# A selective-scan kernel whose work between two batches is put out by a model of the engines

## The chip, the cores and the metric

The kernel runs on one core of a Trainium2 chip. Its time is the device time of one execution in microseconds (us); the runs shown of before have a median of 16161.84 us. A core has a matrix engine (TensorE, PE in the profile), three elementwise engines (VectorE or DVE, ScalarE or ACT, GpSimd or POOL) and a queue that issues most transfers (SyncE, SP). Each engine takes its instructions in the order of its own program.

## The reference: what is computed

The input x is (4, 64, 64, 96): four images of L = 4096 positions and 96 channels. Four layers follow each other, and the change touches the first two, which have the same skeleton:

```
xg   = GroupNorm(x)                       # 32 groups of 3 channels
xi,z = split(xg @ in_proj_w.T)            # 192 channels each
xc   = silu(depthwise_conv3x3(xi) + b)
for each of 4 directions kd:              # four orders of the 4096 positions
    dt, B, C = projections of xc in that order
    h[t] = h[t-1] * exp(dt[t] * A) + dt[t] * xc[t] * B[t]     # 192 channels x 16 states
    y_kd[t] = sum over states of h[t] * C[t], plus D * xc[t]
y = sum over kd of w_kd * y_kd, brought back to the image's order
y = LayerNorm(y over the 192 channels) * ln_g + ln_b
y = y * silu(z)
```

Layer 0 walks the image along diagonals and by radius, with weights w_kd for each position, and ends with `x + y @ out_proj_w.T`. Layer 1 walks rows and columns, forwards and backwards, without weights; its y goes on to an out-projection and a feed-forward block. Layers 2 and 3 (attention, a quantised feed-forward, an FFT mixer) are not touched.

## The kernel before, in words

All arithmetic is in f32. `Stream.run` treats the first two layers as one row of eight batches (two layers times four images). A batch is 4 directions of 4 segments of 1024 positions, each of 6 channel blocks and 4 groups of states. The steady work of a batch is: VectorE enters (line 725) and scans (line 732), ScalarE takes exponentials (L720), GpSimd multiplies by C (L742), and TensorE gathers over states (`collect`, L753) and spreads the inputs (L712). Idle matmuls on zeros (`keep_busy`, L776) lie ahead of the collects; they write the column tile that the collect's first part writes too, and the collect's second part writes another tile.

Before a batch can be scanned, its **front** must have run (`front`, from L259): it loads the image in strips of 1024 positions, takes GroupNorm statistics (L284 on VectorE, L291 and L297 on TensorE), loads the strips again, normalises them (L310), and for each of the four strips projects the inner half by channels (L318, copied to a padded tile at L324), projects z by tokens (L330, Silu at L335, stored to `z_tok`), convolves (L356), applies Silu (L370), transposes to tokens (L376, copies L380), stores `x_tok` (L391) and the product with D's weights `dx_tok` (L393 on GpSimd, store L398).

The convolution is 108 matmuls of 32x32 weights (diagonals) with 512 columns for each strip: 9 taps, 3 blocks of 32 channels in each half, and 4 positions `at` (two halves times two groups of 8 rows). `tile_position=(blk * 32, at * 32)`: the block picks the row group of the matrix array and the position the column group.

After a batch has been scanned, its **merge** runs (`merge`, from L407) in 8 chunks of 512 positions: it fetches the four directions' y (L422 by SP, or L426 by 64 indirect transfers of GpSimd, for directions 2 and 3 of layer 0), sums them (L448 with weights, L450 without), takes LayerNorm statistics (L460, L461), applies norm and affine and multiplies by z, in rows of tokens (L472 to L474 on VectorE in layer 0; in layer 1 VectorE normalises at L478 and GpSimd does three passes, L480 and L481), transposes (L492), copies (L497 on ScalarE), and then projects and adds x (L504, L506; layer 0) or stores `y1` (layer 1).

Between batch q-1 and batch q no scan runs: `flush` ends the last collects, and then `between(q)` puts out front(q+1) and merge(q-1), step by step in turn, with the front left out in every third turn. Only after that the program spreads the inputs of batch q (`spread_u`, L712) and scans on. The order in each engine's program is exactly the order in which these generators put it out (`manual_schedule`); nothing moves it later. SP and GpSimd issue transfers in that order too, so a transfer that waits for its data holds the ones behind it.

At the start the order is: front(0) alone, then the fetch of the first segment (`fetch`, L559, 52 transfers) and its preparation (`prepare`, L605 to L690), the loads of the first rows of B, C and delta, then `between(0)`, which is front(1) alone, then the first scan. At the end merge(7) runs alone.

Of the kernel before, what the change touches and what calls it, by code (L numbers as in the profile page):

```python
# [21 lines left out]
B = 4  # L22
# [122 lines left out]

class Layer:


    def __init__(self, s, a, pre, x_in):
# [9 lines left out]
        self.ln_g, self.ln_b = (k.t(w, [128, DI], pre + n) for n in ("ln_g", "ln_b"))  # L159
        nc.sync.dma_start(self.ln_g, a[pre + "ln_g"].to_broadcast([128, DI]))  # L160
        nc.sync.dma_start(self.ln_b, a[pre + "ln_b"].to_broadcast([128, DI]))
# [58 lines left out]
class Stream:  # L220
# [38 lines left out]
    def front(self, bt):  # L259

        k, nc, lay = self.k, self.nc, bt.lay
        x = lay.x_in[:, bt.b, :]
        bt.x_tok = k.t(self.dram, [L, DI], "x_tok")
        bt.dx_tok, bt.z_tok = (k.t(self.dram, [L, DI], n, bufs=3) for n in ("dx_tok", "z_tok"))
        stats = k.t(self.tmp, [C, NCH, 6], "gn_stats")
        strips = L // SEG
        tiles, pads = {}, {}

        def load(s):
            xs = k.t(self.core, [C, SEG], "da", bufs=4)  # L270
            nc.sync.dma_start(xs, x[:, s * SEG : (s + 1) * SEG])
            return xs

        def load_strip(s):

            tiles[s] = load(s), k.t(self.tmp, [C, 2, HW], "halo", bufs=2)
            for n, row in enumerate((s * 16 - 1, s * 16 + 16)):
                if 0 <= row < HW:
                    nc.sync.dma_start(tiles[s][1][:, n], x[:, row * HW : (row + 1) * HW])

        for c in range(strips):
            xs = load(c)
            for j in range(2):
                nc.vector.bn_stats(stats[:, 2 * c + j, :], xs[:, j * CH : (j + 1) * CH])  # L284
            yield
        for s in range(2):
            load_strip(s)
        mv, gn, d = (k.t(self.tmp, [C, n], t) for n, t in ((2, "gn_mv"), (2, "gn"), (1, "gn_d")))
        nc.vector.bn_aggr(mv, stats.rearrange("p c s -> p (c s)"))
        ps = k.t(self.ps, [C, 1], "m")  # L290
        nc.tensor.matmul(ps, self.gavg, mv[:, 0:1], start=True, stop=True)  # L291
        yield
        nc.vector.tensor_copy(gn[:, 0:1], ps)
        nc.vector.tensor_sub(d, mv[:, 0:1], gn[:, 0:1])
        nc.vector.scalar_tensor_tensor(d, d, d, mv[:, 1:2], op0=ALU.mult, op1=ALU.add)
        ps = k.t(self.ps, [C, 1], "m")
        nc.tensor.matmul(ps, self.gavg, d, start=True, stop=True)  # L297
        yield
        k.rstd(gn[:, 1:2], ps)

        def project(s):

            pad = pads[s] = self.spare()[:C].rearrange("p (h r w) -> p h r w", h=2, r=18)
            nc.gpsimd.memset(pad[:, :, :, 0 : HW + 2 : HW + 1], 0.0)
            r0 = s * 16
            xs, halo = tiles.pop(s)
            has = [r0 > 0, r0 + 16 < HW]
            edge = slice(0 if has[0] else 1, 2 if has[1] else 1)
            for v in (xs, halo[:, edge]):
                nc.vector.tensor_scalar(v, v, gn[:, 0:1], gn[:, 1:2], op0=ALU.subtract, op1=ALU.mult)  # L310
            for n in range(2):
                if not has[n]:
                    nc.gpsimd.memset(pad[:, :, n * 17, :], 0.0)
            for part in range(3):
                v = xs[:, part * CH : (part + 1) * CH] if part < 2 else halo[:, edge].rearrange("p r w -> p (r w)")
                ps = k.t(self.ps_t, [C, 2, CH], "t")[:, :, : v.shape[1]]
                for half in range(2):
                    nc.tensor.matmul(ps[:, half], lay.in_w[:, half * C : (half + 1) * C], v, start=True, stop=True)  # L318
                yield
                if part < 2:  # L320
                    rows = slice(1 + part * 8, 9 + part * 8)
                else:
                    rows = slice(edge.start * 17, 18, 17) if edge.stop == 2 else slice(0, 1)
                nc.scalar.copy(pad[:, :, rows, 1 : 1 + HW], ps.rearrange("p h (r w) -> p h r w", w=HW))  # L324
            stores = []
            for j in range(2):
                ps = k.t(self.ps_t, [128, 2, CH], "t")[:, :, : 2 * DI].rearrange("p a (b d) -> p a b d", d=DI)
# [12 lines left out]
            for to, z in stores:  # L340
                nc.sync.dma_start(to, z)
# [1661 lines left out]
```

## Time and profile before

| | us |
|---|---|
| runs shown: median (lowest to highest) | 16161.84 (16144.28 to 16188.49) |
| the profiled execution's own time | 16120.49 |
| its span | 16118.7 |
| first scan (L732) begins | 392.5 |
| gaps without a scan between batches 0-1, 1-2, 2-3, 3-4 (merge of layer 0) | 206.8, 206.4, 209.0, 209.5 |
| gaps 4-5, 5-6 (merge of layer 1, front of layer 1) | 187.1, 185.0 |
| gap 6-7 (merge alone) | 129.8 |
| last scan ends | 12878.7 |
| granted TensorE clock, mean of the span | 0.861 |

The share of busy time over the whole span is PE 83%, DVE 80%, POOL 62%, ACT 51%. It is an average over stages with different limits, so the gaps and the start are read by themselves, by the busy time in stretches. A matmul in f32 is two passes of the array in the records, and each is counted as one instruction.

### The profile page before, as it was taken

What the parts mean: (1) busy time and instruction counts of PE and PEld (TensorE: products, weight loads), DVE (VectorE), ACT (ScalarE), POOL (GpSimd) and SP (SyncE); (2) the same over time, 40 slices, a digit from 0 to 9 for tenths busy, and PEclk for the clock granted to TensorE, in tenths of its full rate; (3) what the DMA queues carried; (4) which work ended last, traced back from release to release, by engine and by line L of the source; (5) the groups of instructions that cost most, each with busy time, mean ns of one, the idle gap of its engine ahead of it and who ended that gap; (6) DMA issues with size and microseconds to landing.
All of it is one profiled execution on the core that took longest, in us unless ns stands there. A gap on an engine that the chain in (4) does not pass through costs nothing. (4 is left out here: it accounts for less than half of the span.)

```text
span 16118.7 us, 190118 instructions
## 1 busy us (share of the span) xinstructions
PE 13409.0 (83%) x70447; PEld 4873.8 (30%) x70447; DVE 12944.4 (80%) x9690; ACT 8242.0 (51%) x14120; POOL 9957.1 (62%) x5025
## 2 busy tenths in 40 slices
PE   6888788878887888788878887888688869998877
PEld 3222222222222222222222222222222234443344
DVE  1989798979897989799979997999899956565555
ACT  3656465646564656466545654655466523332334
POOL 1888588858885888577757775777677730000123
PEclk8888888988888888888878888888788879998878
DMA  3333533353334333433343334333433320000132
GB/s 113 107 114 109 157 109 110 114 160 104 115 107 151 107 115 109 152 109 119 115 143 120 111 114 154 107 115 107 139 112 122 101 65 18 11 17 13 37 84 69
DMA packets 927836, 1675.23 MB, mean 104 GB/s; under 512 B 103206, under 2 KB 617515, under 8 KB 923132
## 3 DMA queue, kind: packets, MB, share of 16 engines
q1 hardware_dynamic: 890044, 1587.51, 31.7%
q0 software_dynamic: 36864, 75.55, 1.5%
q8 instruction: 558, 9.14, 0.2%
q14 instruction: 370, 3.03, 0.1%
HBM read 1308.00 MB, written 354.75 MB: 103 GB/s over the span
## 5 line engine op out<-in xcount | busy, mean ns | idle before, releaser
L742 POOL TENSOR_TENSOR hc<-h,bc 128x1024 f32<-128x1024 f32 x3072 | 7183.5, 2357 | 2112.6 <-DVE h L732 1681.4
L732 DVE TENSOR_TENSOR_SCAN h<-da,state,t 128x1024 f32<-128x1024 f32 x2304 | 5270.8, 2328 | 13.7 <-ACT da L720 9.6
L753 PE MATMUL y<-hc,gather_y 128*32 128x512 f32 x12288 | 4281.9, 689 | 671.4 <-POOL hc L742 506.2
L725 DVE TENSOR_TENSOR t<-u,bc 128x1024 f32<-128x1024 f32 x3072 | 3599.5, 1217 | 998.8 <-PE u L712 998.3
L720 ACT ACTIVATE da<-dts,L_A_logs 128x1024 f32<-128x1024 f32 x3072 | 3488.1, 1147 | 730.8 <-DMA dts<-dt_dram 438.4
L712 PE MATMUL u<-dtu,spread 32*128 32x512 f32 x3072 | 1881.2, 739 | 374.2 <-DVE t L725 370.2
L776 PE MATMUL y<-L_diag,zeros 96*32 96x256 f32 x5218 | 1751.8, 466 | 0.0
L732 DVE TENSOR_TENSOR_SCAN h<-da,t 128x1024 f32<-128x1024 f32 x768 | 1711.7, 2268 | 9.1 <-ACT da L720 8.4
L753 PEld LDWEIGHTS y<-hc,gather_y 128*32 128x32 f32 x12288 | 802.1, 117 | 2465.9 <-issue 1266.7
L644 PE MATMUL m<-xs,proj 96*128 96x512 f32 (+1 forms) x2048 | 1017.8, 620 | 116.7 <-ACT dt L653 60.4
L681 ACT COPY dt<-m 96x512 f32<-96x512 f32 x512 | 296.7, 579 | 1533.5 <-PE m L676 1533.5
L712 PEld LDWEIGHTS u<-dtu,spread 32*128 32x128 f32 x3072 | 597.9, 215 | 1440.1 <-issue 1101.2
L776 PEld LDWEIGHTS y<-L_diag,zeros 96*32 96x32 f32 x5218 | 617.7, 132 | 1284.8 <-issue 1158.4
L1186 POOL MEMSET padp<- 128x2448 f32 x32 | 68.5, 2141 | 1413.1 <-PE d L1226 1405.0
L1262 DVE SCALAR_TENSOR_TENSOR hcv<-padv,taps,hcv 128x2048 f32<-128x2048 f32 x384 | 902.2, 2349 | 22.3 <-ACT padv L1203 8.6
L1226 PE MATMUL d<-padp,diag 32*32 32x512 f32 x25600 | 886.2, 601 | 2.0 <-ACT hcp L1241 2.0
L676 PE MATMUL m<-sp_z,ident 96*96 96x512 f32 x1024 | 535.1, 605 | 192.7 <-ACT sp_z L670 192.7
L636 POOL TENSOR_TENSOR dtu<-sp_z,dtu 96x1024 f32<-96x1024 f32 x256 | 604.1, 2360 | 72.5 <-ACT dtu L634 70.1
L648 ACT ACTIVATE sp_z<-m,L_dtb 96x512 f32<-96x512 f32 x512 | 348.8, 681 | 545.4 <-PE m L644 527.7
L1226 PEld LDWEIGHTS d<-padp,diag 32*32 32x32 f32 x25600 | 483.3, 103 | 372.1 <-issue 199.3
L797 ACT COPY spare<-m 128x512 f32<-128x512 f32 x384 | 225.0, 586 | 713.3 <-PE m L794 712.9
L644 PEld LDWEIGHTS m<-xs,proj 96*128 96x128 f32 (+1 forms) x2048 | 322.6, 177 | 822.8 <-issue 314.2
(276 smaller groups left out, 15542.6 us busy)
## 6 DMA issues: line engine op xcount, KB each, us to landing
bc<-bc_dram SPq DMA_DIRECT2D x1024, 512.0 KB
dts<-dt_dram SPq DMA_DIRECT2D x768, 512.0 KB
dt_dram<-dt SPq DMA_DIRECT2D x256, 384.0 KB
h<-y_tok SPq DMA_DIRECT2D x192, 384.0 KB
y_tok<-spare SPq DMA_DIRECT2D x64, 768.0 KB
z_tok<-z_rows SPq DMA_DIRECT2D x64, 384.0 KB
x_tok<-y_rows SPq DMA_DIRECT2D x32, 768.0 KB
dx_tok<-sp_z SPq DMA_DIRECT2D x32, 768.0 KB
```

The source lines that it names most:

```text
L636: rest = lambda half: nc.gpsimd.tensor_add(r[:, half], z[:, half], r[:, half])
L644: nc.tensor.matmul(ps, proj[:, src, to], xs[:, src, cols], start=src == 0, stop=src == 1)
L676: nc.tensor.matmul(ps, k.ident[:C, :C], term[:, half, cols], start=at == 0, stop=at == 2)
L712: self.nc.tensor.matmul(seg.u[:, cols], self.spread[rows, :], seg.dtu[rows, half, cols], start=True, stop=True)
L720: self.nc.scalar.activation(da, seg.dts[cb], AF.Exp, scale=seg.bt.lay.neg_a[:, seg.kd, g : g + 1])
L725: self.nc.vector.tensor_mul(gr.t, gr.seg.u, self.bc[:, 0, gr.sg, :])
L732: self.nc.vector.tensor_tensor_scan(gr.h[:, order], gr.da[:, order], gr.t[:, order], start, op0=ALU.mult, op1=ALU.add)
L742: self.nc.gpsimd.tensor_mul(gr.hc, gr.h, self.bc[:, 1, gr.sg, :])
L753: nc.tensor.matmul(seg.y[at : at + GC, :], self.gather_y, gr.hc[:, part * CH : (part + 1) * CH], start=gr.sg == 0, stop=gr.sg == NSG - 1, ...
L776: self.nc.tensor.matmul(gr.seg.y[at : at + GC, :256], self.zeros, gr.seg.bt.lay.diag.rearrange("p h t c -> p (h t c)")[:, :256], start=Fal ...
L1226: nc.tensor.matmul(pc[i][j * 32 : (j + 1) * 32, :], diag[mine, ON_PE.index(t), tap, :], pad[mine, j * 8 + dy : j * 8 + dy + 8, dx : dx + H ...
L1262: nc.vector.scalar_tensor_tensor(to, win, wt, to, op0=ALU.mult, op1=ALU.add)
```

## The change

`between` is replaced by `side_by_side`. Fronts and merges become many small threads that tell, before each step, which engine it needs and for how many microseconds by the code's own table (`yield "PE", 2.7`). `Plan.run` keeps for each engine the time at which the model has it free, and puts out next the thread that can start first. `Rings` keeps count of the buffers. Where the model sees TensorE idle for over 1 us it puts in an idle matmul of 384 columns (`fill`). The flush of the last collects is itself a thread (`ending`), at 1.2 us of the model's time, and fetches of directions 0 and 1 may stand ahead of it; they land in the halves of the tiles "dt" and "xs" of the segments, which hold z as well.

Five more things change with it. At the start, front(0) and front(1) are put out together, ahead of the first segment's fetch and preparation. A front loads the image once and keeps its four strips. z is projected by channels (two matmuls of 96x512 for each half strip, stored to `z_t` as [96, 2, L]). The convolution's loops go block, tap, position, and each block is one step of the plan. In the merge, VectorE normalises, the transposed result gets the affine on ScalarE (`Identity` with scale and bias for each channel), and the product with z follows by channels on VectorE. The pad's borders are cleared by VectorE. ln_g and ln_b are loaded as [96, 2].

```diff
+class Plan:
...
+    def run(self):
+        now = 0.0
...
+                start = max(th.at, self.free.get(th.wants[0], 0.0))
+                if best is None or (start, -th.ahead) < (best[0], -best[1].ahead):
+                    best = start, th
+            start, th = best
+            engine, us = th.wants
+            if engine == "PE" and self.fill:
+
+                for _ in range(int((start - self.free.get("PE", start)) / 1.0)):
+                    self.fill()
+            if engine != "none":
+                self.free[engine] = start + us
+                now = max(now, start)
+            th.at = start + us + (0.2 if us else 0.0)
+            self.current = th
+            th.wants = next(th.work, None)
+            if th.wants is None:
+                self.threads.remove(th)
+        self.current = None
...
-    def front(self, bt):
+    def front(self, bt, plan, rings, first=None):
...
+        if first:
+            yield lambda: first.to_project == 0
+        bt.to_project = L // SEG
...
+        bt.dx_tok = k.t(self.dram, [L, DI], "dx_tok", bufs=3)
...
+        mv, gn, d = (k.t(self.tmp, [C, n], t, bufs=2) for n, t in ((2, "gn_mv"), (2, "gn"), (1, "gn_d")))
+
+        def measure(s, st):
+            st.x = yield from take(self.core, [C, SEG], "da", 4)
+            yield "SP", 0.1
+            nc.sync.dma_start(st.x, x[:, s * SEG : (s + 1) * SEG])
+            yield "none", 2.5
+            yield "DVE", 1.4
+            for j in range(2):
+                nc.vector.bn_stats(stats[:, 2 * s + j, :], st.x[:, j * CH : (j + 1) * CH])
...
+        yield from plan.together([measure(s, st) for s, st in enumerate(strips)])
+        yield "DVE", 0.4
         nc.vector.bn_aggr(mv, stats.rearrange("p c s -> p (c s)"))
...
-        def project(s):
...
-            nc.gpsimd.memset(pad[:, :, :, 0 : HW + 2 : HW + 1], 0.0)
...
+        def project(s, st):
+
+            whole = yield from take(self.w, [128, 2 * 18 * (HW + 2)], "spare", 2)
+            pad = whole[:C].rearrange("p (h r w) -> p h r w", h=2, r=18)
...
+            xs, halo = st.x, st.halo
+            yield "DVE", 2.2
+            nc.vector.memset(pad[:, :, :, 0 : HW + 2 : HW + 1], 0.0)
+            for n in range(2):
+                if not has[n]:
+                    nc.vector.memset(pad[:, :, n * 17, :], 0.0)
             for v in (xs, halo[:, edge]):
                 nc.vector.tensor_scalar(v, v, gn[:, 0:1], gn[:, 1:2], op0=ALU.subtract, op1=ALU.mult)
-            for n in range(2):
-                if not has[n]:
-                    nc.gpsimd.memset(pad[:, :, n * 17, :], 0.0)
...
+                yield "ACT", 1.1 if part < 2 else 0.4
                 nc.scalar.copy(pad[:, :, rows, 1 : 1 + HW], ps.rearrange("p h (r w) -> p h r w", w=HW))
-            stores = []
-            for j in range(2):
-                ps = k.t(self.ps_t, [128, 2, CH], "t")[:, :, : 2 * DI].rearrange("p a (b d) -> p a b d", d=DI)
-                for t in range(4):
-                    at = j * CH + t * 128
-                    nc.tensor.matmul(
...
-                    )
...
+            def outer(j):
+                cols = slice(j * CH, (j + 1) * CH)
+                ps = yield from take(self.ps_t, [C, 2, CH], "t", 2)
+                yield "PE", 1.8
+                for half in range(2):
+                    w = lay.in_w[:, DI + half * C : DI + (half + 1) * C]
+                    nc.tensor.matmul(ps[:, half], w, xs[:, cols], start=True, stop=True)
+                z = yield from take(self.tmp, [C, 2, CH], "z_rows", 2)
+                yield "ACT", 1.1
                 nc.scalar.activation(z, ps, AF.Silu)
-                at = r0 * HW + j * CH
-                to = bt.z_tok[at : at + CH, :].rearrange("(j p) d -> p j d", p=128)
-                stores.append((to, z.rearrange("p a b d -> p (a b) d")))
-            yield
...
+                give(ps)
+                del ps
+                yield "SP", 0.1
+                at = s * SEG + j * CH
+                nc.sync.dma_start(bt.z_t[:, :, at : at + CH], z)
...
+            yield from plan.together([inner(part) for part in range(3)])
+            st.pad, st.whole = pad, whole
+            del pad, whole
+            yield from plan.together([outer(j) for j in range(2)])
...
+        def convolve(s, st):
+            yield lambda: st.pad is not None
...
+            two = yield from take(self.ps_t, [128, 2, CH], "t", 2)
+            one = yield from take(self.ps, [128, CH], "m", 1)
             ps = [two[:, 0, :], two[:, 1, :], one]
-            for tap in range(9):
-                dy, dx = divmod(tap, 3)
-                for blk in range(C // GC):
-                    mine = slice(blk * GC, (blk + 1) * GC)
+            for blk in range(C // GC):
+                yield "PE", 2.7
+                mine = slice(blk * GC, (blk + 1) * GC)
+                for tap in range(9):
+                    dy, dx = divmod(tap, 3)
                     for at in range(4):
                         half, j = divmod(at, 2)
                         nc.tensor.matmul(
                             ps[blk][at * GC : (at + 1) * GC, :],
                             lay.diag[mine, half, tap, :],
-                            pad[mine, half, j * 8 + dy : j * 8 + dy + 8, dx : dx + HW],
+                            st.pad[mine, half, j * 8 + dy : j * 8 + dy + 8, dx : dx + HW],
                             start=tap == 0,
                             stop=tap == 8,
                             tile_position=(blk * GC, at * GC),
                         )
-
-            for _ in range(3):
-                yield
-            xc = []
+            give(st.whole)
+            del st.whole, st.pad
...
+                yield "ACT", 0.7
                 nc.scalar.activation(xc[blk], ps[blk], AF.Silu, bias=lay.conv_b[:, blk : blk + 1])
...
             for blk, ps in enumerate((two[:, 0, :], two[:, 1, :], one)):
+                yield "PE", 1.2
                 for t in range(4):
                     nc.tensor.transpose(ps[:, t * 128 : (t + 1) * 128], xc[blk][:, t * 128 : (t + 1) * 128], k.ident)
...
+                yield "ACT", 0.8
                 for half in range(2):
...
-                nc.gpsimd.tensor_mul(dx, dx, rows)
+                nc.gpsimd.tensor_mul(dxs, dxs, flat)
...
-            for _ in range(3):
...
-        for s in range(strips + 1):
-            if s < strips:
-                yield from project(s)
-            if s:
-                yield from convolve(s - 1)
-
-
-    def merge(self, bt):
+                nc.gpsimd.tensor_mul(dxs, flat, lay.weight_x.unsqueeze(1).to_broadcast([128, SEG // 128, DI]))
...
+        works = [work for s, st in enumerate(strips) for work in (project(s, st), convolve(s, st))]
+        yield from plan.together(works)
+
+
+    def merge(self, bt, plan, rings):
...
+        whole = k.t(self.seg, [128, 2, SEG], "dt")
+        rings.parts("rows", [whole[:, i, : T * DI].rearrange("p (j d) -> p j d", d=DI) for i in range(2)])
+        whole = k.t(self.seg, [C, 2, SEG], "xs")
+        rings.parts("z", [whole[:, i].rearrange("p (h t) -> p h t", h=2) for i in range(2)])
+
+        def fetch(kds):
+            if kds[0]:
+                yield lambda: self.ended
+            for n in range(NCH):
+                for kd in kds:
+                    if kd < 2:
+                        g = yield from take(None, None, "rows", 2)
+                    else:
+                        g = yield from take(self.core, [128, T, DI], "h", 4)
+                    if not lay.ordered or kd < 2:
+                        yield "SP", 0.1
+                        nc.sync.dma_start(g, rows_of(bt.y_tok[kd], n))
...
+                            )
+                    plan.add(landed((n, kd), g))
...
+        def finish(n, acc, mv):
+            plan.add(load(("z", n), None, None, "z", 2, bt.z_t[:, :, cols_of(n)]))
+            yield "ACT", 1.0
+            nc.scalar.activation(mv[:, :, 1], mv[:, :, 1], AF.Sqrt, bias=k.eps)
+            yield "DVE", 1.7
+            nc.vector.reciprocal(mv[:, :, 1], mv[:, :, 1])
             for j in range(T):
...
+                m, r = mv[:, j, 0:1], mv[:, j, 1:2]
+                nc.vector.tensor_scalar(acc[:, j], acc[:, j], m, r, op0=ALU.subtract, op1=ALU.mult)
+            give(mv)
+            ps = yield from take(self.ps_u, [C, 2, CH], "u", 1)
             if lay.ordered:
...
-                nc.vector.tensor_mul(acc, acc, z.pop())
...
-                nc.gpsimd.tensor_mul(acc, acc, z.pop())
...
+                plan.add(load(("x", n), tmp, [C, CH], "x_in", 1, lay.x_in[:, bt.b, cols_of(n)]))
+            yield "PE", 2.4
...
-            yt = k.t(tmp, [C, 2, CH], "yt")
-            nc.scalar.copy(yt, ps)
...
+            yt = yield from take(tmp, [C, 2, CH], "yt", 1)
+            yield "ACT", 1.4
+            for half in range(2):
+                g, b = lay.ln_g[:, half : half + 1], lay.ln_b[:, half : half + 1]
+                nc.scalar.activation(yt[:, half], ps[:, half], AF.Identity, bias=b, scale=g)
+            yield lambda: ("z", n) in got
+            z = got.pop(("z", n))
+            yield "DVE", 1.1
+            nc.vector.tensor_mul(yt, yt, z)
...
             if not lay.ordered:
...
+                give(ps)
+                yield "SP", 0.1
+                nc.sync.dma_start(self.y1[:, bt.b, cols_of(n)].rearrange("(h c) t -> c h t", c=C), yt)
...
+            yield "PE", 1.6
...
-    def between(self, q, batches):
...
-        turn = 0
-        while work:
-            turn += 1
-            for one in list(work):
-                if len(work) == 2 and one is work[0] and turn % 3 == 0:
-                    continue
-                if next(one, self) is self:
-                    work.remove(one)
...
+        yield from plan.together([fetch((0, 1)), fetch((2, 3)), sums()])
...
+    def side_by_side(self, ahead, behind=None, flush=None):
...
+        def ending():
+
+            yield "none", 1.2
+            if flush:
+                flush()
+            self.idle = k.t(self.ps_y, [128, CH], "y")
+            self.ended = True
+            yield "PE", 4.0
+
+        def fill():
+            if self.idle is not None:
+                data = self.layers[0].diag.rearrange("p h t c -> p (h t c)")[:, :384]
+                nc.tensor.matmul(self.idle[:GC, :384], self.zeros, data, start=True, stop=True)
+
+        plan.fill = fill
+        if behind:
+            plan.add(self.merge(behind, plan, rings))
+        for bt in ahead:
+            plan.add(self.front(bt, plan, rings, None if bt is ahead[0] else ahead[0]), 1)
+        plan.add(ending())
+        plan.run()
+        self.idle = None
...
         with k.tc.manual_schedule():
-            for _ in self.front(batches[0]):
-                pass
+            self.side_by_side(batches[:2])
             self.fetch(segs[0])
             self.run_hooks(len(self.hooks), len(self.runs))
             weave.start(self.prepare(segs[0]))
...
                 if first_of(slots[n]):
-                    flush()
+                    q = batches.index(seg.bt)
+                    if q:
+                        self.side_by_side(batches[q + 1 : q + 2], batches[q - 1], flush)
                     before = []
                     seg.bt.y_tok = [k.t(self.dram, [L, DI], f"y_tok{kd}") for kd in range(ND)]
-                    self.between(batches.index(seg.bt), batches)
...
-            flush()
-            for _ in self.merge(batches[-1]):
-                pass
+            self.side_by_side([], batches[-1], flush)
```

## The prediction

> **What bounds the kernel now.** I read first the page's bar of 40 slices and then the busy time by stretches. The scan part is eight batches with the VectorE full, and between them stretches in which no scan runs. All of the change lies in these stretches and in the start. The table lists them; its columns are span, then busy time and instructions of TensorE, its weight loads, VectorE, ScalarE and GpSimd, then granted TensorE clock, DMA share and GB/s.
>
> ```profile
> core 0: us, PE busy (x) PEld busy (x) DVE busy (x) ACT busy (x) POOL busy (x), PEclk, DMA share, GB/s
> 0.00:392.40 392.40, 264.94 (x2324) 147.33 (x2324) 41.17 (x105) 120.98 (x255) 39.42 (x31) 0.85 0.38 114
> 1806.70:2013.50 206.80, 118.51 (x1150) 63.75 (x1150) 110.52 (x304) 59.95 (x92) 87.43 (x75) 0.75 0.65 192
> ...
> 8224.00:8411.10 187.10, 104.72 (x1120) 61.64 (x1121) 86.88 (x159) 59.45 (x92) 65.31 (x36) 0.71 0.66 200
> ...
> 11391.50:11521.30 129.80, 26.44 (x93) 15.84 (x94) 80.10 (x139) 18.33 (x26) 51.36 (x26) 0.52 0.64 197
> ```
>
> First scan at 392.4; four gaps like the second row (206.8, 206.4, 209.0, 209.5), two like the third (187.1, 185.0), one of 129.8, and a last merge from 12878.7 on. In the large gaps no engine is full: TensorE is busy 57%. So they are bounded by hand-overs, and an order that overlaps more could gain, if no engine gets more work.
>
> Second view: the convolution, the largest piece of TensorE work, first as its tile's instructions, then as they start in time (start us, us, engine, line).
>
> ```profile
> L356 PE MATMUL t<-spare,L_diag x144: 584/587/612, 1888.0 to 1895.6; 32*32 32x512 f32 x144
> L356 PE MATMUL m<-spare,L_diag x72: 585/587/612, 1888.1 to 1895.8; 32*32 32x512 f32 x72
> ```
>
> ```profile
> 1888.02 0.66 PE L356 MATMUL t<-spare,L_diag 32*32 32x512 f32 x8 [1.02 <-ACT z_rows L335]
> 1888.08 0.63 PE L356 MATMUL m<-spare,L_diag 32*32 32x512 f32 x4
> 1888.45 0.66 PE L356 MATMUL t<-spare,L_diag 32*32 32x512 f32 x8
> 1888.53 0.61 PE L356 MATMUL m<-spare,L_diag 32*32 32x512 f32 x4
> 1888.88 0.85 PE L356 MATMUL t<-spare,L_diag 32*32 32x512 f32 x8
> ```
>
> A strip is 216 passes (108 matmuls of two) in 18 waves of 12, one pass on each of 12 array tiles (three row groups by four column groups). Waves start 0.43 us apart: a tile is held 0.4275 us by a pass of 512 columns, and 12 tiles work side by side. 18 waves and the drain are 8.36 us.
>
> Third view: does TensorE run ahead past passes that wait for a busy tile? During scans, idle matmuls on one column tile (L776) are followed by collects (L753), half on that tile and half on another.
>
> ```profile
> 1049.12 2.36 POOL L742 TENSOR_TENSOR hc<-h,bc 128x1024 f32<-128x1024 f32 x1
> ```
>
> ```profile
> 1053.92 3.19 PE L776 MATMUL y<-L_diag,zeros 96*32 96x256 f32 x7
> 1056.49 1.06 PE L753 MATMUL y<-hc,gather_y 128*32 128x512 f32 x1
> 1056.91 0.63 PE L776 MATMUL y<-L_diag,zeros 96*32 96x256 f32 x1
> ```
>
> The data of the collect were there at 1051.48 (GpSimd's last product), and its second tile was free; yet its first pass started at 1056.49, when all but one of the idle passes ahead of it had started. So passes are handed out in order, and only some three can wait at a busy tile before everything behind stands still.
>
> Fourth, the start: fetch and preparation of the first segment come before the second front.
>
> ```profile
> 202.68 0.36 SPq L398 DMA_DIRECT2D dx_tok<-sp_z  x1
> 203.09 20.39 SPq L559 DMA_DIRECT2D x_got<-x_tok  x52
> ```
>
> ```profile
> 115.00:200.00 85.00, 72.54 (x1024) 44.15 (x1024) 3.65 (x8) 31.14 (x57) 11.54 (x7) 0.98 0.48 145
> ...
> 298.00:390.00 92.00, 79.63 (x1032) 47.43 (x1032) 5.37 (x14) 34.56 (x61) 13.59 (x7) 0.87 0.46 139
> ...
> 275.00:298.00 23.00, 0.00 (x0) 0.00 (x0) 4.92 (x8) 0.32 (x1) 1.97 (x4) 0.52 0.98 319
> ```
>
> Front(0) 115.4 to 203.1 (88), preparation 71.3 to 274.4, loads of the first B/C and delta rows at DMA share 0.98 to 298 (24), front(1) until the scan at 392.4.
>
> **The change part by part.**
>
> *Convolution order.* Tap, block, position becomes block, tap, position. Twelve consecutive matmuls now lie on four tiles, not twelve. By the two views above a block takes 18 waves of 0.4275 = 7.7 us, three blocks 23.1 instead of 8.4: +14.7 us of TensorE time per strip, +59 per front, on all 32 strips. (If a next block, directly behind, starts in the three waiting passes, it is 2 x 4 x 0.4275 = 3.4 less, 19.7; in the new program other matmuls mostly lie between.) The plan books 2.7 us for a block, so what it places around them comes late.
>
> [...]
>
> *Rest of the front on TensorE, per strip.* Projection 8 passes x 0.4275 = 3.42 and its halo 0.25 as before; z by channels again 8 passes, 3.42 (by tokens it was 2 x 1.43 = 2.9: +0.5); transposes 12 x 0.11 = 1.3. Sum 31.5, 126 per front (before 65). GroupNorm loads x once instead of twice (4 loads less on SP per front, 0.6 us of issue each, no longer between statistics and projection); pad memsets move from GpSimd to VectorE (4 x below 1.6, the normalisation's row).
>
> *Merge.* Out go, layer 0, on VectorE two affine passes (32 x 0.41 + 32 x 0.42 = 26.4 per gap) and ScalarE's copy (1.0); layer 1 three GpSimd passes of some 2 us a chunk (48 per gap). In come 32 normalisations on VectorE (some 0.31, as layer 1's now), two ScalarE passes of 0.68 (+0.35 a chunk), and the product by z by channels, 1.1 on VectorE (layer 0 had 0.97). Gathers on GpSimd are unchanged: 64 indirect DMAs, 73 us, and 4 x 3.5 of multiplication, 87 in all, starting some 13 us into the gap; they end long before TensorE. Directions 0 and 1 are fetched into the halves of two segment tiles, ahead of the flush; what SP has queued behind the last y store (issued 7.4 us into the gap) is the first x load, as before.
>
> *Layer 0 gap.* First projection: before 44 us into the gap (1850.7). The new order puts two directions' sums ahead of the group's reciprocal instead of all four: 36 (ends: 25, the statistics' loads alone; 44). Then TensorE: front 126, merge 8 x (8 x 0.11 + 4 x 0.4275) = 21, fills 1 = 148; in-order waits for copies, gates and z stores some 14 (before, 163 us from the first projection on held some 107 of busy time): 162; over the clock. The dense fronts above had 0.98 and 0.87; I take 0.94: 173. Gap 36 + 173 = 209 against 207.9 on average: +1.5. Ends: 187 (25 + 148 + 14 at full clock) and 227 (44 + 162/0.885). Four gaps: +6.
>
> *Layer 1 gap.* No out-projection: 126 + 7 + 1, waits 15, = 149; / 0.94 = 158.5; + 33 = 191.5 against 186. +5.5, twice: +11.
>
> *Merge alone, twice.* TensorE has little; GpSimd's three passes leave the chunk's path, VectorE gets the product (8 x 1.1) and ScalarE the affine. Now a chunk comes every 12.9 us with VectorE busy 10. I take 11.8 for it: -9 each (ends -30, VectorE without waits after the first 11 us at full DMA, and +5, the product exposed). -18.
>
> *Start.* Both fronts now precede fetch and preparation. SP takes orders in turn, so the 52 fetches wait behind front(1)'s last dx store. F = time from the first projection to that store: TensorE 252, GroupNorm of front(1) and the last strip's tail (Silu, transposes, copies, stores, 3.4 us of GpSimd) some 26, in-order waits 18: 296. Then preparation 71, loads 24, first scan some 2 later. Before: 88 + 71 + 118 = 277 from 115.4. After: F + 97 = 393: +116. Ends: F = 266 (busy time and tail) +86; F/0.87 = 340, +163. What was hidden: front(1) covered the 24 us of loads with 92 of its own; now nothing covers them, nor the preparation.
>
> Sum: 6 + 11 - 18 + 116 = +115 on a profiled execution of 16120.5 (span 16118.7): 16235. That execution lies 41 us below the median of the runs shown, 16161.8; against this the forecast is **16277**.
>
> **Rivals.**
>
> *B: blocks overlap, faster.* If four more tiles start while a block runs, convolution stays 8.4. TensorE in a layer 0 gap is 148 - 59 = 89, the gap between 36 + (89 + 14)/0.94 = 146 and today's; I take 162: -45 x 4; layer 1 150: -36 x 2; merges -18; start F = 2 x 88 + 11, + 7. Sum about -260: 15900. For it: large gaps with idle engines. Against: the L776 rows. It decides from the point where a strip's three blocks take under 15 us together.
>
> *C: slower still.* Four busy tiles, or the waits that the plan misjudges by 5 us a block, keep the clock at 0.87 or add in-order waits: layer 0 gaps 227, layer 1 as much longer, start +163, merges as before: 4 x 19 + 2 x 21 + 163 = +281: 16443. For it: the clock was 0.50 from 1815 to 1856, 0.64 to 1880. Against: denser TensorE work had 0.98.
>
> *D: about unchanged or a little faster.* The hand-overs vanish in full: gaps at their floors (187 and 25 + 134 + 14 = 173: -21 x 4, -13 x 2), merges -20 each, start +86: -64; half of the way there from the forecast: +25, near 16190. It needs several floors at once.
>
> **How the numbers follow.** Forecast 0.62 (its own range 16190 to 16370), C 0.15, D 0.14, B 0.09. 0.3% is 48 us, about what a measurement of this kernel tells from no change. Faster by more: B and a third of D, 0.13; within: the rest of D and the forecast's low edge, 0.14; slower 0.73. The range reaches from D's near side to C: 16115 to 16445, leaving out B and D's floor.
>
> **What would show it.** L356's successor: 36 matmuls of a block as 18 waves of four, 7.7 us a block, TensorE busy over 155 in a layer 0 gap and scans from 505 on. Wrong if a strip's blocks start 0.1 us apart, if the fetch of the first segment starts before 380, or if gaps fall below 185.

## The result

The changed kernel takes 17059.54 us (median, 17023.57 to 17079.24) against 16175.17 us of the kernel before, measured beside it (16144.28 to 16197.54). The ratio is 1.0546, with a 95% interval of 1.0517 to 1.0574. It is slower, as forecast, but by 884 us where 115 were forecast, and outside the range of 16115 to 16445.

The page of the changed kernel's profiled execution begins as follows (span and instructions; busy time, share and instructions of each engine; then the slices' granted clock):

```profile
span 17077.5 us, 190088 instructions
...
PE 14851.2 (87%) x70659; PEld 5053.3 (30%) x70659; DVE 12866.4 (75%) x9642; ACT 8303.3 (49%) x14192; POOL 9748.0 (57%) x4881
...
PEclk7688868886888688868886888688888889999878
```

TensorE is busy 1442 us longer than before with practically the same number of instructions, and the clock line now has a 7 and a 6 at the start and a 6 wherever a gap with a front lies. Busy time by stretches of the changed kernel, with the columns of the table before (span, then PE, PEld, DVE, ACT, POOL, granted TensorE clock, DMA share, GB/s); the rows are the start, the first gap with a merge of layer 0, the first with a merge of layer 1, and the gap with a merge alone:

```profile
core 0: us, PE busy (x) PEld busy (x) DVE busy (x) ACT busy (x) POOL busy (x), PEclk, DMA share, GB/s
0.00:697.70 697.70, 591.99 (x2340) 183.76 (x2340) 41.84 (x117) 123.75 (x254) 37.53 (x19) 0.66 0.20 60
...
2117.50:2427.40 309.90, 279.45 (x1147) 82.72 (x1148) 101.36 (x277) 68.38 (x109) 82.88 (x70) 0.61 0.44 127
...
8964.80:9250.90 286.10, 256.18 (x1122) 76.58 (x1122) 79.89 (x174) 65.52 (x99) 16.74 (x6) 0.61 0.43 125
12361.00:12468.80 107.80, 64.77 (x184) 23.39 (x184) 66.71 (x146) 21.01 (x34) 2.78 (x2) 0.74 0.81 235
```

In the first layer 0 gap TensorE went from 118.5 busy of 206.8 us to 279.5 of 309.9: it is the bound now, at a clock of 0.61 instead of 0.75. The difference of the two profiled spans, 958.8 us, adds up like this:

| part | before | after | difference |
|---|---|---|---|
| start, to the first scan | 392.5 | 697.7 | +305.3 |
| four gaps with a merge of layer 0 | 831.7 | 1249.9 | +418.2 |
| two gaps with a merge of layer 1 and a front | 372.2 | 580.1 | +207.9 |
| gap with a merge alone | 129.8 | 107.8 | -22.0 |
| the eight batches | 11152.7 | 11222.6 | +69.9 |
| after the last scan | 3240.0 | 3219.2 | -20.8 |

Starts and gaps that hold a front make up 931 of it. The 70 us in the batches themselves are not explained: they sum to 11153 and 11164 in the profiles of the two kernels with the old order by turns, and to 11177 to 11253 in those with the new plan.

What happens inside is read from the convolution's rows. The first view is TensorE in time during the first front's second strip (start us, us, engine, line), where two blocks follow each other directly:

```profile
162.16 1.08 PE L482 MATMUL m<-spare,L_diag 32*32 32x512 f32 x4
162.99 1.08 PE L482 MATMUL t<-spare,L_diag 32*32 32x512 f32 x4
163.01 1.08 PE L482 MATMUL m<-spare,L_diag 32*32 32x512 f32 x4
163.84 1.08 PE L482 MATMUL t<-spare,L_diag 32*32 32x512 f32 x4
163.87 1.08 PE L482 MATMUL m<-spare,L_diag 32*32 32x512 f32 x4
164.69 1.08 PE L482 MATMUL t<-spare,L_diag 32*32 32x512 f32 x4
164.72 13.02 PE L482 MATMUL m<-spare,L_diag 32*32 32x512 f32 x60
```

Two things are to be seen. The next block (m) starts at 162.16, three waves ahead of the last wave of the block before it (t, 164.69), and no earlier: this agrees with three passes waiting at a tile, as the prediction read it from the idle matmuls. But a wave takes 0.83 to 0.85 us, not 0.43. The second view is the granted clock in short stretches of the first strip's first block and of a later pair of blocks:

```profile
133.40:136.00 2.60, 2.60 (x25) 0.77 (x28) 0.00 (x0) 1.01 (x1) 0.00 (x0) 1.00 0.00 0
136.00:146.00 10.00, 10.00 (x52) 2.33 (x44) 0.00 (x0) 0.00 (x0) 0.00 (x0) 0.50 0.01 2
```

```profile
207.00:234.00 27.00, 27.00 (x145) 6.05 (x144) 0.00 (x0) 2.29 (x3) 0.00 (x0) 0.50 0.16 45
```

In this profile blocks run in 86 stretches of one or two. The 31 stretches that start at full clock have their first 6 to 13 waves 0.43 us apart and fall to half within 2.5 to 5.8 us, although TensorE is busy without a break; the other 55 start at half. Single blocks of 18 waves take 9.9 to 15.6 us, and what follows a block runs at half clock too. The projection by four matmuls, 1.96 us ahead of a block, takes 3.73 behind it:

```profile
2221.04 1.96 PE L445 MATMUL t<-da,L_in_wT 96*96 96x512 f32 x4 [0.67 <-ACT z_rows L448]
...
2238.24 3.73 PE L445 MATMUL t<-da,L_in_wT 96*96 96x512 f32 x4
```

### The profile page after: what moved, and what is told of

The parts are those of the page before. It is cut to its first block, busy times and chain, and to the rows that moved or that the text cites. A ratio compares the mean times of both kernels' runs of the same rounds, so it can differ in the third digit from the quotient of the medians.

```text
span 17077.5 us, 190088 instructions
## 1 busy us (share of the span) xinstructions
PE 14851.2 (87%) x70659; PEld 5053.3 (30%) x70659; DVE 12866.4 (75%) x9642; ACT 8303.3 (49%) x14192; POOL 9748.0 (57%) x4881
## 5 line engine op out<-in xcount | busy, mean ns | idle before, releaser
L482 PE MATMUL t<-spare,L_diag 32*32 32x512 f32 x4608 | 880.5, 944 | 1.5 <-ACT z_rows L448 1.5
L844 PE MATMUL m<-dt,ident 96*96 96x512 f32 x1024 | 564.5, 633 | 4.6 <-ACT dt L849 2.0
```

The lines of the kernel that those rows point to most:

```text
L482: nc.tensor.matmul(ps[blk][at * GC : (at + 1) * GC, :], lay.diag[mine, half, tap, :], st.pad[mine, half, j * 8 + dy : j * 8 + dy + 8, dx : ...
L844: nc.tensor.matmul(ps, k.ident[:C, :C], term[:, half, cols], start=at == 0, stop=at == 2)
```

## The experiments

The theory after the result has two parts: block order makes the waves of a strip three times as many (54 instead of 18), and with one row group of the array at work the clock is halved (0.50 in the rows above). Its rivals: the loss lies in the plan's order as such; the clock falls for another reason (idle time, the serial order); it falls with the number of tiles at work rather than with the rows.

### The convolution's order alone, both ways

The changed kernel with the old loop order, as one step of the plan:

```diff
-            for blk in range(C // GC):
-                yield "PE", 2.7
-                mine = slice(blk * GC, (blk + 1) * GC)
-                for tap in range(9):
-                    dy, dx = divmod(tap, 3)
+            yield "PE", 8.4
+            for tap in range(9):
+                dy, dx = divmod(tap, 3)
+                for blk in range(C // GC):
+                    mine = slice(blk * GC, (blk + 1) * GC)
                     for at in range(4):
```

> The changed kernel with one edit: the convolution's loops go tap, block, position again, as one step of the plan. Theory (the loss is the convolution's order: a block keeps four array tiles at work, and the TensorE clock falls while it runs): a strip takes 8.4 us again, the granted clock in a gap is 0.75 or more, layer 0 gaps 145 to 170 us, first scan at 375 to 410, the kernel at about 15900 us, below before. Rival (the loss lies in the plan's order itself, its hand-overs and its start): the convolution is quick again but the gaps stay above 200 us and the kernel above before.

Measured: 16029.02 us against 16185.31, ratio 0.9885 (0.9847 to 0.9922). The first scan begins at 408.1. The layer 0 gaps are 192.6, 195.6, 177.3 and 179.1, the layer 1 gaps 169.4 and 166.5, the merge alone 104.2. Its stretches, the start and a gap of each kind:

```profile
0.00:408.10 408.10, 296.79 (x2318) 139.54 (x2318) 49.42 (x117) 121.93 (x254) 37.66 (x19) 0.86 0.34 102
1805.20:1997.80 192.60, 141.72 (x1170) 62.23 (x1170) 100.84 (x277) 68.70 (x110) 82.99 (x70) 0.81 0.70 208
...
8181.00:8350.30 169.30, 116.60 (x1118) 55.15 (x1118) 82.63 (x173) 61.69 (x97) 17.76 (x6) 0.80 0.72 211
```

With one loop order undone, the whole loss is gone and a gain of 1.15% is left. The theory's gaps (145 to 170) were too short for layer 0, and so was its time; the rival's (above 200) are not reached.

And the kernel before with the new loop order only:

```diff
-            for tap in range(9):
-                dy, dx = divmod(tap, 3)
-                for blk in range(C // GC):
-                    mine = slice(blk * GC, (blk + 1) * GC)
+            for blk in range(C // GC):
+                mine = slice(blk * GC, (blk + 1) * GC)
+                for tap in range(9):
+                    dy, dx = divmod(tap, 3)
                     for at in range(4):
```

> The kernel before with one edit: the convolution's loops go block, tap, position. Theory: a strip takes 35 to 43 us instead of 8.4, and since the convolution stands on TensorE's own chain this shows nearly in full: layer 0 gaps about 325 us, the two fronts of the start 120 us more each, the kernel about 17100 us. Rival (the new order costs only together with the plan): gaps below 230 us, kernel within 1% of before.

Measured: 17083.72 us, ratio 1.0560 (1.0536 to 1.0585). First scan at 615.3, layer 0 gaps 322.6 to 330.0 (granted clock 0.59 in the first), layer 1 gaps 304.4 and 304.2. The loop order alone makes as much loss in the old kernel as the whole change does (898 and 884 us). The plan has no part in it.

### The clock held up by zeros

The changed kernel in block order, with matmuls of zero weights beside each of a block's matmuls, so that every wave has 12 tiles again:

```diff
                         half, j = divmod(at, 2)
+                        for other in range(C // GC):
+                            if other != blk:
+                                rows = slice(other * GC, (other + 1) * GC)
+                                nc.tensor.matmul(
+                                    ps[other][at * GC : (at + 1) * GC, :],
+                                    self.zeros[rows, :],
+                                    st.pad[rows, half, j * 8 + dy : j * 8 + dy + 8, dx : dx + HW],
+                                    start=other > blk,
+                                    stop=other > blk or (blk == 2 and tap == 8),
+                                    tile_position=(other * GC, at * GC),
+                                )
...
-                            stop=tap == 8,
+                            stop=blk == 2 and tap == 8,
```

> The changed kernel, block order kept; beside each of a block's matmuls two matmuls with zero weights run on the same column group of the two other row groups, so that 12 tiles work in every wave (the zeros are added to the other blocks' sums and change nothing). Theory (few working tiles bring the clock down): the clock stays up, a block is 18 waves of 0.43 us, 7.7 us, a strip 23 us, layer 0 gaps near 209, first scan near 508, the kernel near 16280, what the prediction gave. Rival 1 (the clock falls for idle time ahead of the blocks or for the serial order): waves still 0.85 us apart after the first ones, kernel near 17060. Rival 2 (the extra matmuls cost dispatch time): waves longer than 0.43 us at a full clock.

Measured: 16426.75 us, ratio 1.0155 (1.0131 to 1.0179). Two strips of the start, each over most of its length:

```profile
167.50:194.00 26.50, 26.50 (x652) 16.17 (x652) 0.07 (x1) 1.25 (x2) 3.47 (x1) 1.00 0.40 120
...
377.00:403.00 26.00, 26.00 (x651) 16.19 (x650) 0.00 (x0) 1.11 (x2) 3.47 (x1) 1.00 0.31 94
```

Three times the matmuls, and the clock is 1.00, waves are 0.43 us, and the kernel is 633 us faster than the changed one. So adding work that computes nothing removes 633 of the loss. The remaining 398 against tap order go with the 54 waves in place of 18 (36 waves of 0.43 us on 32 strips would be some 490 if all of it showed). Both parts of the theory hold. With the clock up, the prediction's first scan (508) and layer 0 gap (209) are nearer to what is measured, but still too low: 540.4, and 218.5 to 231.2; for layer 1 it had 191.5, and 221.3 and 223.7 are measured.

### Rows or tiles

The position outermost: three tiles at a time, one in each row group, against four tiles in one row group.

```diff
-            for blk in range(C // GC):
-                yield "PE", 2.7
-                mine = slice(blk * GC, (blk + 1) * GC)
+            for at in range(4):
+                yield "PE", 2.1
                 for tap in range(9):
                     dy, dx = divmod(tap, 3)
-                    for at in range(4):
+                    for blk in range(C // GC):
+                        mine = slice(blk * GC, (blk + 1) * GC)
```

> The changed kernel with the loops position, tap, block: three tiles at a time, in three row groups and one column group, against four tiles in one row group. A strip is 4 x 18 waves. If the clock goes by the number of working tiles, it falls here too: waves 0.855 us, a strip about 60 us, kernel about 17600. If it goes by the rows of the array that work, it stays up: waves 0.43, a strip 31 us, kernel about 16520, faster than the changed kernel although a strip takes four thirds of its waves.

Measured: 16571.21 us, ratio 1.0239 (1.0206 to 1.0272), faster than the changed kernel with a third more waves. Two strips:

```profile
174.00:205.00 31.00, 31.00 (x225) 9.29 (x225) 0.34 (x1) 2.08 (x5) 3.42 (x1) 1.00 0.34 104
361.00:391.00 30.00, 30.00 (x221) 8.96 (x220) 0.34 (x1) 1.67 (x3) 3.42 (x1) 1.00 0.35 107
```

Three tiles at a time instead of block order's four, and a clock of 1.00 instead of 0.50: here the number of tiles is not what counts. Two row groups together and then one alone tell how many are needed:

```diff
-            for blk in range(C // GC):
-                yield "PE", 2.7
-                mine = slice(blk * GC, (blk + 1) * GC)
+            for some in ((0, 1), (2,)):
+                yield "PE", 2.7 * len(some)
                 for tap in range(9):
                     dy, dx = divmod(tap, 3)
-                    for at in range(4):
+                    for blk in some:
+                        mine = slice(blk * GC, (blk + 1) * GC)
+                        for at in range(4):
...
```

> The changed kernel with the convolution in two steps: blocks 0 and 1 together by taps (eight tiles in two row groups), then block 2 alone (four tiles in one). Three row groups held the full clock with three tiles as with twelve, one row group did not. If two are enough, the waves of the first step stay at 0.43 us and only the second step falls to 0.85; if not, both do. At full clock in the first step a strip is 7.7 + some 12, first scan near 535, layer 0 gaps near 225; at half clock in both a strip is some 27, first scan near 570, gaps near 245.

Measured once: 16391.64 us. One strip in three stretches: the first step, the projection that lies between with the second step's first waves, and the rest of the second step.

```profile
199.80:207.40 7.60, 7.60 (x145) 2.59 (x144) 0.00 (x0) 0.65 (x2) 3.44 (x1) 1.00 0.62 201
207.60:211.00 3.40, 3.40 (x28) 1.07 (x24) 0.00 (x0) 1.31 (x2) 0.00 (x0) 1.00 0.17 29
211.00:222.00 11.00, 11.00 (x64) 2.52 (x56) 0.00 (x0) 0.86 (x2) 0.00 (x0) 0.57 0.21 67
```

With two row groups (64 rows) 18 waves take 7.96 us at a clock of 1.00; with one, the clock falls (0.57 from 211 to 222) and 18 waves take 12.7. Of the 32 first steps in this profile, 28 ran at 1.00 throughout. Three others met the half rate at their start or within 0.8 us and stayed there for the whole 15 us. One of them:

```profile
10159.20:10174.70 15.50, 15.50 (x145) 3.69 (x144) 13.28 (x22) 3.45 (x6) 3.95 (x1) 0.50 0.81 249
```

So in this run two row groups kept a clock of 1.00 for the 8 us of a step, but did not bring it back within 15 us. The old order with its 12 tiles on three row groups started at half 7 times in the profile of the kernel before, and had the full clock back after 1.7 to 8.0 us. Longer stretches on two row groups, and fewer tiles on them, weren't tried. First scan at 532.8, layer 0 gaps 220.7 to 230.0, as expected for the first case.

### The other terms

The start put back (front(1) after the preparation), with tap order:

```diff
-            self.side_by_side(batches[:2])
+            self.side_by_side(batches[:1])
...
-                    if q:
-                        self.side_by_side(batches[q + 1 : q + 2], batches[q - 1], flush)
+                    self.side_by_side(batches[q + 1 : q + 2], batches[q - 1] if q else None, flush)
```

> The kernel with the convolution's loops tap, block, position, and the start put back: front(0), then fetch and preparation of the first segment, then front(1) and the first scan. With tap order and both fronts first, the first scan begins at 408.1, before at 392.5. If putting both fronts first leaves preparation and loads without cover, the first scan comes 15 us earlier, at 385 to 395, and the kernel is 15 us faster than with tap order alone, about 16010 us. Rival (the start's loss is elsewhere, in the fronts' own order by threads): first scan stays at 405 or later.

Measured: 16033.58 us, ratio 0.9918 (0.9896 to 0.9939); first scan at 405.8. The rival was right. Of the 16 us that the first scan is later than before with both fronts first, the start's order is worth 2. The other 13 stand in the old order too, because the first front is itself later (in this run its first projection at 125 instead of 115.4, its last store at 214 instead of 203).

The convolution in tap order, but cut into three steps of the plan:

```diff
-            yield "PE", 8.4
             for tap in range(9):
+                if tap % 3 == 0:
+                    yield "PE", 2.8
```

> The kernel with the convolution's loops tap, block, position, but as three steps of the plan with three taps each (2.8 us) instead of one of 8.4, so that the plan may put other TensorE work between, as block order allowed. If finer steps are worth something to the merges beside, layer 0 gaps fall from 186 on average by 5 us or more. If the gaps are bounded by loads and the fronts' own chain, they stay within 4 us.

Measured: 16032.73 us, ratio 0.9907 (0.9882 to 0.9932). Layer 0 gaps 184.3, 179.1, 180.5, 179.6 (mean 181, 5 less), layer 1 gaps 177.8 and 178.3 (10 more): no gain on the whole.

Without the plan's idle matmuls, with tap order:

```diff
-        plan.fill = fill
```

> The kernel with the convolution's loops tap, block, position, and without the idle matmuls that the plan puts in. If they only take TensorE's time, gaps fall by a few us. If they keep the clock up, the granted clock of a gap falls below 0.78 and gaps grow; with 18 fills of 0.3 to 0.7 us and only ahead of work that the model sees late, the effect stays within 5 us a gap.

Measured: 16023.99 us, ratio 0.9901 (0.9877 to 0.9925), layer 0 gaps 184.3 to 194.3, layer 1 165.4 and 171.1. On the whole the fills neither cost nor help, but two effects lie behind that. Without them the granted clock of the gaps with a front is 0.72 to 0.78, with them 0.78 to 0.88: they do hold it up. And they take TensorE's time where the first projection is due. Without them it comes 35.8 to 37.1 us into a gap instead of 37.1 to 40.1, and the first scan begins at 396.1 instead of 408.1, near the 392.5 of before. At the start, the last fills ahead of the first projection (tap order alone), and the first projection without fills:

```profile
118.92 5.11 PE L697 MATMUL y<-L_diag,zeros 96*32 96x384 f32 x8
```

```profile
116.70 3.73 PE L429 MATMUL t<-da,L_in_wT 96*96 96x512 f32 x4 [1.50 <-DVE da L421]
```

With fills the projection begins at 124.0, directly behind those 5.1 us; without them it waits 1.5 us for its data. One profile of each shows this, and GroupNorm's statistics, ahead of both, were 4 us earlier in the run without fills, so not all of the 12 us need be the fills'. The four kernels with tap order so far are all about 1% faster than the kernel before, and can't be told apart.

The merge alone became 21 to 26 us shorter in the kernels with the new plan, where 9 were forecast. Three GpSimd passes are put back into layer 1's merges (multiplications by one, where before there were gain, bias and gate):

```diff
+        self.ones = k.t(w, [128, DI], "ones_row")
+        nc.gpsimd.memset(self.ones, 1.0)
...
             give(mv)
+            if not lay.ordered:
+                for _ in range(3):
+                    yield "POOL", 2.0
+                    nc.gpsimd.tensor_tensor(acc, acc, self.ones.unsqueeze(1).to_broadcast([128, T, DI]), ALU.mult)
```

> The kernel with the convolution's loops tap, block, position, and in layer 1's merges three GpSimd passes over each chunk added again (multiplications by one, where before GpSimd did gain, bias and gate). It tells apart what made the gap with a merge alone 104 us instead of 130. If it is the GpSimd passes, by their place in the chunk's chain and because VectorE's additions took 1515 ns beside them and 958 without, the gap goes back to 120 or more and the additions to 1400 ns or more. If it is the earlier fetches (directions 0 and 1 ahead of the flush) and their order, the gap stays below 110.

Measured once: 16146.84 us, beside 16266.77 for the kernel before; the merge alone takes 124.5 us. Rows of that gap (line, engine, operation, count, busy, mean ns of one), in the kernel before, then with tap order and no GpSimd passes, and then with them:

```profile
L450 DVE TENSOR_TENSOR hc<-hc,h 128x768 f32<-128x768 f32 x24 | 36.4, 1515 | 2.1 <-DMA h<-y_tok 1.4
```

```profile
L607 DVE TENSOR_TENSOR hc<-hc,h 128x768 f32<-128x768 f32 x16 | 15.3, 958 | 0.5
```

```profile
L637 POOL TENSOR_TENSOR hc<-hc,ones_row 128x768 f32<-128x768 f32 x24 | 57.5, 2397 | 56.7 <-DVE hc L632 55.5
...
L609 DVE TENSOR_TENSOR hc<-hc,h 128x768 f32<-128x768 f32 x16 | 25.7, 1605 | 0.3
L657 DVE TENSOR_TENSOR yt<-yt,xs 96x1024 f32<-96x1024 f32 x8 | 16.3, 2041 | 9.9 <-ACT yt L653 9.9
```

And the additions one by one (duration minimum, median, maximum in ns):

```profile
L609 DVE TENSOR_TENSOR hc<-hc,h x16: 946/958/2448, 11411.3 to 11492.6; 128x768 f32<-128x768 f32 x16
```

The gap goes from 104.2 back by 20, most of the way to 129.8. With the passes of 2.4 us on GpSimd, VectorE's additions take 958 ns in the median and up to 2448, 1605 on average; without the passes the mean is 958, and in the kernel before it was 1515. So most of the merge's gain, 20 of 26 us, is the GpSimd passes: their place in the chunk's chain, and VectorE's longer additions beside them. How it divides between the two wasn't separated.

One thing in this run stays open. Its layer 0 gaps, whose operations the edit doesn't touch, are 207.8 to 213.0 instead of 177 to 196; in the first of them the convolution's rows are busy 98.6 us instead of 67.8, and its weight loads idle 32 us for nothing that the profile shows, instead of 8. What makes the difference wasn't tried.

## Why the prediction was wrong, point by point

- **Convolution order: the waves were right, the clock was not.** The number of waves (18 for each block) and their order (three waves of overlap, where blocks follow directly) are as read from the L776 rows. The step that failed is "over the clock. The dense fronts above had 0.98 and 0.87; I take 0.94". The granted clock was 0.61 in the gap and 0.50 within the blocks. The dense fronts that gave 0.98 and 0.87 ran with three row groups. In the prediction's sum, the 162 us of TensorE over 0.61 instead of 0.94 are 266, and the gap 302, against 306 to 319 measured. For layer 1, 149 / 0.61 + 33 = 277, against 286 and 294. That one factor carries most of the miss: of the 769 us between forecast and result (884 against 115), 633 went when zeros held the clock up. Smaller terms make up the rest. The fills were put at 1 us of TensorE in a layer 0 gap and were busy 13.8 in the first; the batches grew by 70, which the sum did not hold. Two slips in the sums are of no weight: 162 / 0.94 is 172, and 209 against 207.9 is 1.1.
- **First projection:** put at 36 us in layer 0 gaps, measured 37.0 to 39.3: nearly right. In layer 1 gaps the sum had 33, measured 39.8 and 40.0: 7 too low.
- **Start.** F was put at 296, 252 of it TensorE at full clock; measured 485 (124.5 to 609.3). The 252 over the clock of those stretches, 0.61 up to 400 us and 0.56 from there, and the 44 beside it, give 457 to 494. F began at 124.5 instead of 115.4, 9 later, and from the fetch to the first scan the sum had 97, and 88 were measured. The reading that the old order covered the preparation and the loads was wrong: in the prediction's own row from 275 to 298 TensorE is busy 0.00 beside the loads, so they stood alone before, too, and with tap order the two orders of the start differ by 2 us (408.1 and 405.8). The +116 of the sum comes from F: 296 for what took 88 and 94 before. Its upper end, with F / 0.87, is +160 and not +163.
- **Merge alone, -9 each:** right in sign, too small: -22 (-26 with tap order), and -21 after the last scan. The term took the chunk's pace from GpSimd's place in the chain and left out that VectorE's own additions (1515 ns in the row of before) become 958 without GpSimd beside them.
- **Rival B** (blocks overlap, 15900 us) fell as a mechanism: in the changed kernel each of the ten stretches of two blocks took 27.56 us, the second starting three waves ahead of the first one's last and no earlier. But its sum was a forecast of tap order: 16029 measured, 129 above. Layer 0 gaps of 186 on average instead of 162 make most of that.
- **Rival C** named four busy tiles as a danger to the clock and priced it at 0.87, since nothing lower stood in the dense rows. Rows at 0.50 were there, from 1815 to 1856 of the profile before, but beside a TensorE that was busy 6.25 of the 41 us. The end of the range rested on the wrong bound.
- **Rival D** needed every floor at once; only that of the merges (-20) was reached.

## What to carry to other kernels

When array tiles are used separately, interleave the matmuls so that the row groups work at the same time: here a block at a time, on one row group of 32, made 54 waves of a strip's 18 and brought the granted clock to 0.50, for itself and for what came after (a projection of 1.96 us took 3.73). Ahead of a reordering on TensorE, price both terms, waves and clock, and when no row shows the new pattern at work, bound the clock from below by the lowest that the profile shows anywhere (0.50 here). And a pass taken off GpSimd can be worth more than its place in a chain: look at what VectorE's two-operand instructions cost beside it (here 1515 ns with the passes of before and 958 without).

## What was not expected of the hardware

- The granted clock went to half with TensorE busy without a break, when the matmuls used 32 of the array's rows (four tiles in one row group): 0.50 over 27 us. With 64 rows (eight tiles) it stayed at 1.00 through 28 of 32 steps of 8 us, but three steps that met the half rate were at 0.50 to the end, 15 us later. With 96 rows, in three tiles or twelve, it was 1.00 over the 26 to 31 us of the rows shown. So in these runs it went with the rows and not with the number of tiles or of instructions, and rows with zero weights counted too (1.00 over 26.5 us).
- The fall came 2.5 to 5.8 us after a block that had started at 1.00 began. Behind it, four matmuls that took 1.96 us ahead took 3.73.
- VectorE's additions of two 128x768 tiles in the merge alone took 958 ns on average without GpSimd passes, and 1605 (up to 2448) with three passes of 2397 ns a chunk put back.
